# Seven block products for q G in a linear attention, added to x as their banks grow

## The chip, the cores and the metric

The kernel runs on one core of a Trainium2 chip. The metric is the device time of one execution in microseconds. An execution has five engines with queues of their own: PE (TensorE, matrix products, with a separate row PEld for its weight loads), DVE (VectorE), ACT (ScalarE), POOL (GpSimd) and SP (SyncE, which here issues DMAs).

## The reference

Four layers in a row on a tensor x of 2 batches, 1024 positions and 512 channels, each with a residual sum and a normalization of rows: a linear attention, a gated feed-forward network with 4-bit weights, a gated recurrent attention, and a routed feed-forward network. The change lies in the first layer, of which this is the core (16 heads of 32 channels):

```
q = elu(x Wq^T) + 1 ; k = elu(x Wk^T) + 1 ; v = x Wv^T     # per head
kv  = einsum('bhtd,bhte->bhde', k, v)
z   = 1 / (einsum('bhtd,bhd->bht', q, k.sum(axis=2)) + 1e-6)
out = einsum('bhtd,bhde,bht->bhte', q, kv, z)
x   = layernorm(x + out Wo^T)
```

## The kernel before, in words

Rows of x are cut into four blocks of 512 positions (blocks 0 and 1 are the first batch, 2 and 3 the second); a block is four tiles of 128 rows. All is float32. A tile of 128 rows by 512 columns fills one of the eight PSUM banks.

For each batch `b` the first stage does this. The products x Wk and x Wq of a block are made by `by_seven` (products at L316): a 2 x 2 partition of both operands, seven block products in place of eight, sums of operands on DVE (S1, S2, S3, and T1 to T4 by `sums_of_weights`, L302), and a bank `grow` into which several products are accumulated one after another, read between them. `elu1` (L271 to L273) makes elu + 1 with two passes on ACT and one on DVE. `add_xk` (L367) gathers k^T x in four banks over the two blocks of the batch. `values` (L417) and `G_rows` (L430) turn it into G, a 512 x 512 matrix for which out Wo^T = q G once the rows of q are weighed. `weigh` (L400 to L406) multiplies q's rows by z on DVE. `turned` transposes a weighed tile of q on PE (L197) and copies it to SBUF on ACT (L438). `add_o` multiplies that tile by G with four matmuls of 512 columns (L445), adds the bank to x on DVE (L453) and takes row statistics (L188, L189); after the fourth tile, `layernorm` normalizes the block on POOL (L183). A block of q G is thus four tiles.

Between these, `unpack_some` unpacks 4-bit weights of the second layer piece by piece: a DMA, two shift and mask operations on DVE (L237, L238), then one on ACT into `wgu` (L241) or on DVE into `wdn` (L245). 27 such pieces are spread over the stage. `split_some` transposes tiles of the finished block 0 (L197, `x1Tp`) and splits them in a high part on ACT (L211) and a low part on DVE (L212): the input of the second layer, whose matmuls begin at L632 (`gatep`, `upp`) when the first stage is over.

What runs between what is written by hand. `by_seven` is a generator that stops between products; `run` takes one list of other steps at each stop, and what is left after the last. PE's instructions are held in this written order (`behind`); the order on DVE, ACT and POOL comes from the framework's scheduler when the program is built, and each engine then goes through its instructions in that order. Banks come from rings: `rings["mm"]` (two banks during the stage), `rings["sum"]` (two), `rings["acc"]` (four), and `rings["free"]` for the splits, which is set to the `mm` ring before the last line of steps. The last steps of the stage, for block 3, stand outside of `run`:

```
rings["free"] = rings["mm"]
for more in turns(3, 0, 1) + split[3] + some_o(3, 0) + turns(3, 2) + some_o(3, 1) + turns(3, 3) + some_o(3, 2, 3):
    more()
```

Of the kernel before, what the change touches and what calls it, by code (L numbers as in the profile page):

```python
# [10 lines left out]
F32 = mybir.dt.float32  # L11
# [10 lines left out]
P = 128  # L22
B, T, C = 2, 1024, 512
NB = 4
KC = C // P
# [48 lines left out]
def body(ctx: ExitStack, tc: tile.TileContext, a: dict, out: bass.AP):  # L74
    nc = tc.nc
# [20 lines left out]
    def acc_bank(name):  # L96
        return bank("acc", name)
# [10 lines left out]
    def place_w(i, name):  # L108
        return wpool.tile([P, KC, C], F32, tag=f"A{i}", name=name)
# [4 lines left out]
    x_t = [x[:, :, :C] for x in x_row]  # L114
# [4 lines left out]
    def xT_slot(i, name, dtype=F32):  # L119
        return xtp.tile([P, KC, 512], dtype, tag=f"xT{i}", name=name)  # L120
# [55 lines left out]
    def layernorm(x, mv, eps=1e-5, by=nc.vector):  # L176

        n = x.shape[1]
        rs = sp.tile([P, 4], F32, tag="rs", name="rs")
        nc.vector.tensor_scalar_add(rs[:, :n], mv[:, :, 1], eps)  # L180
        power = nc.gpsimd.tensor_tensor(rs[:, :n], rs[:, :n], const("mhalf")[:, :n], ALU.pow).ins  # L181
        for i in range(n):
            by.tensor_scalar(x[:, i], x[:, i], mv[:, i, 0:1], rs[:, i : i + 1], ALU.subtract, ALU.mult)  # L183
        return power

    def row_stats(mv, x):
        st = sp.tile([P, 6], F32, tag="st", name="st")
        nc.vector.bn_stats(st, x)  # L188
        nc.vector.bn_aggr(mv, st)  # L189
# [98 lines left out]
    def behind():  # L288

        return ExitStack() if last_pe[0] is None else tc.issue_after(last_pe[0])  # L290
# [6 lines left out]
    def sums_of_weights(w, rooms):  # L297

        B11, B12, B21, B22 = (w[:, 2 * e : 2 * e + 2, 256 * o : 256 * o + 256] for e in range(2) for o in range(2))
        T1, T2, T4 = rooms  # L300
        for dst, x, y in ((T1, B12, B11), (T2, B22, T1), (T4, B21, T2), (B12, B22, B12)):
            nc.vector.tensor_sub(dst, x, y)  # L302
        return T1, T2, B12, T4

    def by_seven(x, w, T, rooms, pairs, ready):

        A11, A12, A21, A22 = (x[:, 2 * e : 2 * e + 2, 256 * t : 256 * t + 256] for t in range(2) for e in range(2))
        B11, B12, B21, B22 = (w[:, 2 * e : 2 * e + 2, 256 * o : 256 * o + 256] for e in range(2) for o in range(2))
        T1, T2, T3, T4 = T
        S1, S2, S3 = rooms  # L310

        def product(ps, a, b, first):
            with behind():
                for r in range(2):
                    for k in range(2):
                        ins = nc.tensor.matmul(  # L316
                            ps[:, 256 * r : 256 * r + 256], a[:, k, r * P : (r + 1) * P], b[:, k],
                            start=first and r == 0 and k == 0, stop=k == 1, skip_group_check=True,
                        ).ins
            last_pe[0] = ins  # L320
            return ps.rearrange("p (r c) -> p r c", r=2)

        nc.vector.tensor_add(S1, A21, A22)
        nc.vector.tensor_sub(S2, S1, A11)
        nc.vector.tensor_sub(S3, A11, A21)
        pairs.extend(new_pair(f"pair{t}") for t in range(2))
        c11, c12, c21, c22 = (pairs[t][:, :, 256 * o : 256 * o + 256] for t in range(2) for o in range(2))
        grow = bank("sum", "grow")
        p = product(grow, A11, B11, True)
        nc.scalar.copy(c11, p)  # L330
        yield
        p2 = product(mm_bank("P2"), A12, B21, True)
        nc.vector.tensor_add(c11, c11, p2)
        elu1(c11, c11)
        yield
        product(grow, S2, T2, False)
        nc.scalar.copy(c21, p)
        side = mm_bank("P7")
        p7 = product(side, S3, T3, True)
        nc.vector.tensor_sub(S2, A12, S2)  # L340
        yield
        product(grow, S1, T1, False)
        nc.scalar.copy(c22, p)
        nc.vector.tensor_add(c22, c22, p7)
        elu1(c22, c22)
        yield
        product(grow, S2, B22, False)
        elu1(c12, p)
        ready(0)
        product(side, A22, T4, False)  # L350
        nc.vector.tensor_add(c21, c21, p7)
        elu1(c21, c21)
        ready(1)
# [41 lines left out]
    def weigh(blk, t):  # L395

        for r in range(2):
            x = pairs_of["q", blk][t][:, r]
            e = wk.tile([P, C], F32, tag="e", name="qk")
            nc.vector.tensor_mul(e, x, ksum_of[blk // 2])  # L400
            z = sp.tile([P, 16], F32, tag="z", name="z", bufs=2)
            nc.vector.tensor_reduce(z, e.rearrange("p (h d) -> p h d", d=32), AX.X, ALU.add)
            nc.vector.tensor_scalar_add(z, z, 1e-6)
            nc.vector.reciprocal(z, z)
            x3 = x.rearrange("p (h d) -> p h d", d=32)
            nc.vector.tensor_mul(x3, x3, z.unsqueeze(2).to_broadcast([P, 16, 32]))  # L406

    vkm_of, qT, parts = {}, {}, []

    def values(b):  # L410

# [14 lines left out]
    def G_rows(b):  # L426
        for c in range(KC):
# [2 lines left out]
                last_pe[0] = nc.tensor.matmul(gp, vkm_of[b][:, c], Wo[:, c], start=True, stop=True).ins  # L430
            (nc.scalar.copy if c % 2 else nc.vector.tensor_copy)(G_of[b][:, c], gp)

    def turned(blk, i):
        with behind():
            pt = transposed(pairs_of["q", blk][i // 2][:, i % 2], "qTp", acc_bank)
        last_pe[0] = last_turned[0]
        t = qT[blk, i] = wk.tile([P, KC, P], F32, tag="qT", name="qT")
        nc.scalar.copy(t.rearrange("p k t -> p (k t)"), pt)  # L438

    def add_o(blk, i):  # L440

        ao = acc_bank("ao")
        with behind():
            for k in range(KC):
                ins = nc.tensor.matmul(  # L445
                    ao, qT[blk, i][:, k], G_of[blk // 2][:, k], start=k == 0, stop=k == KC - 1
                ).ins
        last_pe[0] = ins
        x = x_t[blk][:, i]
        if i == 0:  # L450
            mv_of[blk] = sp.tile([P, 4, 2], F32, tag="mv", name="mv")
        mv = mv_of[blk]
        nc.vector.tensor_add(x, ao, x)  # L453
        row_stats(mv[:, i], x)
        if i == 3 and blk < NB - 1:
            layernorm(x_t[blk], mv, by=nc.gpsimd)

    def split_some(*part):
        if 0 in part:
# [39 lines left out]
    def some_xk(blk, *part):  # L499
        return [lambda i=i: add_xk(blk, i) for i in part]  # L500

    def turns(blk, *part):
        return [lambda i=i: turned(blk, i) for i in part]

    def some_o(blk, *part):
        return [lambda i=i: add_o(blk, i) for i in part]

    job = lambda n: [lambda: unpack_some(n)]

    def k_products(blk):  # L510
        return by_seven(xT[blk], Wk, Ts["k"], S_rooms, pairs_of.setdefault(("k", blk), []), lambda t: sum_k(blk, t))

    def q_products(blk):
        return by_seven(xT[blk], Wq, Ts["q"], S_rooms, pairs_of.setdefault(("q", blk), []), lambda t: weigh(blk, t))

    step = lambda f, *x: [lambda: f(*x)]

    for b in range(B):
        i, j = 2 * b, 2 * b + 1
        if b:  # L520
            run(
                k_products(i),
                turns(1, 0, 1),
                some_o(1, 0) + turns(1, 2) + job(1) + some_o(1, 1) + turns(1, 3) + job(1),
                some_o(1, 2) + job(1), some_o(1, 3) + job(1), job(2),
            )
        run(k_products(j), [], some_xk(i, 0, 1) + job(2), some_xk(i, 2) + job(1), some_xk(i, 3) + job(1), job(1 + b))
        if b == 0:
            Ts["q"] = sums_of_weights(Wq, slices(wdn, 0, 3))
        else:  # L530

            Tq = place_w(1, "Tq")
            for n in range(3):
                nc.scalar.copy(Tq[:, n], wdn[:, n])
            Ts["q"] = (*slices(Tq, 0, 2), Ts["q"][2], *slices(Tq, 2, 3))
            S_rooms[0] = pieces_of(Tq[:, 3])
        run(
            q_products(i), [],
            some_xk(j, 0, 1) + job(1), some_xk(j, 2) + step(spread_ksum, b) + job(1), some_xk(j, 3) + job(1 + b),
        )  # L540
        if b == 0:
            xT[2] = load_xT(2)
        split = [step(split_some, n) if b else [] for n in range(4)]
        rings["free"] = (rings["sum"][(turn_of["sum"] + 1) % 2],)
        run(
            q_products(j),
            step(values, b),
            turns(i, 0, 1) + job(1 - b),
            step(G_rows, b) + split[0] + job(1 - b),
            some_o(i, 0) + turns(i, 2) + split[1] + some_o(i, 1) + turns(i, 3) + job(1 - b),  # L550
            some_o(i, 2) + split[2] + some_o(i, 3),
        )
        if b == 0:
            xT[3] = load_xT(3)
    rings["free"] = rings["mm"]
    for more in turns(3, 0, 1) + split[3] + some_o(3, 0) + turns(3, 2) + some_o(3, 1) + turns(3, 3) + some_o(3, 2, 3):
        more()
    late = mv_of[3]
    unpack_some(1000)
# [1025 lines left out]
```

## Time and profile before

| | us |
|---|---|
| median of 3 runs | 990.62 (990.50 to 990.67) |
| the profiled execution | 988.88 |
| its span in the profile | 987.1 |
| granted PE clock, mean | 0.998 |
| PE busy | 972.1 |
| DVE busy | 683.3 |
| the group q G (L445) on PE | 57.3 |

The span is what the profiler saw between the first and last instruction; 1.8 us of the execution lie outside of it. Busy time of an engine is the union of its instructions' durations; durations on PE overlap, so that the distance between starts tells more of a matmul's price than its duration. In the profile, one float32 matmul shows as two passes.

### The profile page before, as it was taken

The numbers are of one execution on the slowest core, as the hardware profiler recorded it, in microseconds if no ns is written. First come the engines' busy times: TensorE is split into PE (matmuls) and PEld (weight loads), VectorE is DVE, ScalarE is ACT, GpSimd is POOL, SyncE is SP. The second block draws the span as 40 slices with busy tenths as digits, with TensorE's granted clock in tenths as the row PEclk, the third lists the DMA queues.
The fourth block names the chain that finished last, engine by engine and source line by source line (L and its number), as shares of the span: only waits on it lengthen the run. The fifth ranks groups of instructions, "written<-read, shape, count | busy, mean of one in ns | idle before, by whom it ended". The sixth has DMA issues, their size and how long they took to land.

```text
span 987.1 us, 11453 instructions
## 1 busy us (share of the span) xinstructions
PE 972.1 (98%) x4253; PEld 745.1 (75%) x4253; DVE 683.3 (69%) x1291; ACT 288.4 (29%) x490; POOL 300.2 (30%) x276
## 2 busy tenths in 40 slices
PE   9999999999999999999999999999999999999996
PEld 6667666756888888888889655776768688888885
DVE  3568877867975686686672465466798795789644
ACT  2244333333542272263240432132220123220000
POOL 1110452004887265575565022002032011000022
PEclk9999999999999999999999999999999999999999
DMA  9632212100000000000020500000004302140011
GB/s 332 200 91 79 72 53 93 37 0 1 1 1 1 1 1 0 2 11 1 1 86 1 220 4 1 1 1 1 1 33 139 128 17 70 43 171 1 1 43 43
DMA packets 25979, 48.84 MB, mean 49 GB/s; under 512 B 4685, under 2 KB 6733, under 8 KB 25412
## 3 DMA queue, kind: packets, MB, share of 16 engines
q1 hardware_dynamic: 23139, 42.85, 13.1%
q0 software_dynamic: 1920, 4.22, 1.1%
q10 hardware_dynamic: 864, 1.05, 0.3%
q8 instruction: 33, 0.54, 0.2%
q14 instruction: 23, 0.18, 0.1%
HBM read 39.70 MB, written 10.52 MB: 51 GB/s over the span
## 4 chain that ended last, share of the span: by engine, by line
PE 84%; issue 8%; DVE 4%; POOL 2%; ACT 1%; DMA 1%; POOLq 0%; ACTq 0%; DVEq 0%
PE P L679 12%; PE yp L1329 9%; PE hp L1250 9%; PE gatep L632 8%; PE upp L632 8%; PE ao L445 6%; PE xk L367 6%; PE grow L316 5%; PE P L316 4%; PE ao L1133 3%; PE go L1089 2%; PE lp L595 1%; PE P L688 1%; PE kp L474 1%; PE up L1006 1%
## 5 line engine op out<-in xcount | busy, mean ns | idle before, releaser
L181 POOL TENSOR_TENSOR rs<-rs,table 128x4 f32<-128x4 f32 (+1 forms) x21 | 18.9, 902 | 327.9 <-DVE rs L180 327.6
L643 DVE SCALAR_TENSOR_TENSOR gate<-gatep,scale,gate 128x512 f32<-128x512 f32 x123 | 91.4, 743 | 7.4 <-PE gatep L632 6.9
L643 DVE SCALAR_TENSOR_TENSOR up<-upp,scale,up 128x512 f32<-128x512 f32 x112 | 83.1, 742 | 0.2
L632 PE MATMUL gatep<-x1Th,wgu 128*128 128x512 f32 x176 | 72.7, 413 | 0.0
L632 PE MATMUL upp<-x1Th,wgu 128*128 128x512 f32 x176 | 69.7, 396 | 0.0
L632 PE MATMUL gatep<-x1Tl,wgu 128*128 128x512 f32 x176 | 69.6, 395 | 0.0
L632 PE MATMUL upp<-x1Tl,wgu 128*128 128x512 f32 x176 | 69.5, 395 | 0.0
L679 PE MATMUL P<-wdn,h 128*128 128x256 f32 x256 | 60.5, 379 | 0.0
L832 POOL TENSOR_TENSOR h<-up,gate 128x512 f32<-128x512 f32 x30 | 38.6, 1287 | 70.4 <-ACT gate L831 65.3
L637 ACT ACTIVATE gate<-gatep,scale 128x512 f32<-128x512 f32 x41 | 28.3, 691 | 106.8 <-PE gatep L632 106.8
L445 PE MATMUL ao<-G,qT 128*128 128x512 f32 x128 | 57.3, 593 | 0.0
L1133 PE MATMUL ao<-W1o,uT 128*128 128x512 f32 x128 | 55.6, 592 | 0.0
L679 PEld LDWEIGHTS P<-wdn,h 128*128 128x128 f32 x256 | 48.5, 190 | 6.7
L1037 POOL TENSOR_TENSOR sum<-sum,sq 128x512 f32<-128x512 f32 x12 | 18.2, 1517 | 107.6 <-issue 83.7
L1133 PEld LDWEIGHTS ao<-W1o,uT 128*128 128x128 f32 x128 | 24.0, 190 | 28.7 <-issue 27.5
L188 DVE BATCH_NORM_STATS2 st<-x 128x6 f32<-128x512 f32 x64 | 42.7, 682 | 0.8
L367 PE MATMUL xk<-pair,x 128*128 128x512 f32 x96 | 42.7, 592 | 0.0
L445 PEld LDWEIGHTS ao<-G,qT 128*128 128x128 f32 x128 | 23.8, 190 | 24.3 <-issue 23.9
L632 PEld LDWEIGHTS upp<-x1Th,wgu 128*128 128x128 f32 x176 | 33.0, 188 | 9.3 <-DVE up L643 1.1
L632 PEld LDWEIGHTS upp<-x1Tl,wgu 128*128 128x128 f32 x176 | 33.1, 188 | 7.6
L632 PEld LDWEIGHTS gatep<-x1Th,wgu 128*128 128x128 f32 x176 | 33.1, 188 | 7.4 <-issue 0.3
L632 PEld LDWEIGHTS gatep<-x1Tl,wgu 128*128 128x128 f32 x176 | 33.1, 188 | 7.1
(405 smaller groups left out, 2239.5 us busy)
## 6 DMA issues: line engine op xcount, KB each, us to landing
pk<-in_gu SPq DMA_DIRECT2D x16, 352.0 KB, 3.7
x<-in_x SPq DMA_DIRECT2D x4, 1024.0 KB, 13.1
w<-in_w SPq DMA_DIRECT2D x1, 4096.0 KB, 16.1
xs<-picked SPq DMA_DIRECT2D x4, 1024.0 KB, 5.0
out<-x SPq DMA_DIRECT2D x4, 1024.0 KB, 4.3
w<-in_w SPq DMA_DIRECT2D x4, 1024.0 KB, 6.3
x0T<-in_xT SPq DMA_DIRECT2D x3, 1024.0 KB, 7.2
pk<-in_dn SPq DMA_DIRECT2D x11, 256.0 KB, 3.3
```

The lines of the kernel that those rows point to most:

```text
L188: nc.vector.bn_stats(st, x)
L316: ins = nc.tensor.matmul(ps[:, 256 * r : 256 * r + 256], a[:, k, r * P : (r + 1) * P], b[:, k], start=first and r == 0 and k == 0, stop=k ...
L367: ins = nc.tensor.matmul(acc_of[b][c], x_t[blk][:, i, c * P : (c + 1) * P], pairs_of["k", blk][i // 2][:, i % 2], start=blk % 2 == 0 and i ...
L445: ins = nc.tensor.matmul(ao, qT[blk, i][:, k], G_of[blk // 2][:, k], start=k == 0, stop=k == KC - 1).ins
L632: ins = nc.tensor.matmul(ps, wgu[:, k, at * P : (at + 1) * P], x[:, k], start=x is parts[0], stop=x is parts[1]).ins
L637: nc.scalar.activation(acc, ps, AF.Copy, scale=s)
L643: last = nc.vector.scalar_tensor_tensor(acc, ps, s, acc, ALU.mult, ALU.add).ins
L679: last_p[0] = nc.tensor.matmul(cut, x(j)[:, r], w[:, j], start=j == 0, stop=j == NP - 1 and tail is None).ins
L832: hm = nc.gpsimd.tensor_mul(h.chunk(f), up, gate).ins
L1133: nc.tensor.matmul(ao[i], uT[blk][:, k, i * P : (i + 1) * P], W1o[:, k], start=n == 0, stop=n == 3)
L1250: nc.tensor.matmul(ps[:, 256 * j : 256 * j + 256], w[:, k, 2 * g + j], x[:, k], start=k == 0, stop=k == 1)
L1329: nc.tensor.matmul(ps[:, 256 * r : 256 * r + 256], x(r, j), w(j), start=j == 0, stop=j == NJ - 1)
```

## The change

Blocks 0, 1 and 2 no longer multiply tile by tile. `turned` keeps q transposed for a whole block, in rooms of `wdn` that are unpacked later (blocks 0 and 1) or in a slot of `xT` (2 and 3). `o_products` then makes q G of the block from seven block products, as `by_seven` does, and adds the growing bank to x after each product: P1 goes to the upper left quarter of x, P1 + P6 to the lower left, and so on. `G_rows` also makes the sums of G. Block 3 stays with four tiles (`add_o`). The weighing of each batch's second block moves from inside its q products to steps after them, three of the four splits of block 0 move into the last line of steps, and unpacking pieces are placed anew.

```diff
     def sums_of_weights(w, rooms):
 
         B11, B12, B21, B22 = (w[:, 2 * e : 2 * e + 2, 256 * o : 256 * o + 256] for e in range(2) for o in range(2))
-        T1, T2, T4 = rooms
-        for dst, x, y in ((T1, B12, B11), (T2, B22, T1), (T4, B21, T2), (B12, B22, B12)):
+        T1, T2, T4, T3 = (*rooms, B12)[:4]
+        for dst, x, y in ((T1, B12, B11), (T2, B22, T1), (T4, B21, T2), (T3, B22, B12)):
             nc.vector.tensor_sub(dst, x, y)
-        return T1, T2, B12, T4
+        return T1, T2, T3, T4
...
@@ G_rows
             (nc.scalar.copy if c % 2 else nc.vector.tensor_copy)(G_of[b][:, c], gp)
 
+        room = wdn[:, 7:11] if b == 0 else place_w(3, "TG")
+        rooms = slices(room, 0, 3)
+        if b:
+
+            rooms.append(pieces_of(wk.tile([P, 512], F32, tag="qT3", name="T3", bufs=1)))
+        TG[b] = sums_of_weights(G_of[b], rooms), pieces_of(room[:, 3])
+
     def turned(blk, i):
+        if i == 0:
+            qT[blk] = wdn[:, 3:7] if blk < 2 else xT_slot(blk % 2, "qT")
...
-        t = qT[blk, i] = wk.tile([P, KC, P], F32, tag="qT", name="qT")
-        nc.scalar.copy(t.rearrange("p k t -> p (k t)"), pt)
+        nc.scalar.copy(qT[blk][:, :, tile_of(i)], pt.rearrange("p (k t) -> p k t", k=KC))
+
+    def o_products(blk):
+
+        A11, A12, A21, A22 = (qT[blk][:, 2 * e : 2 * e + 2, 256 * t : 256 * t + 256] for t in range(2) for e in range(2))
+        G = G_of[blk // 2]
+        B11, _, B21, B22 = (G[:, 2 * e : 2 * e + 2, 256 * o : 256 * o + 256] for e in range(2) for o in range(2))
+        (T1, T2, T3, T4), S1 = TG[blk // 2]
+        S2 = pieces_of(wk.tile([P, 512], F32, tag="qS", name="qS", bufs=1))
+
+        def product(ps, a, b, first, t, o):
+
+            with behind():
+                for r in range(2):
+                    for k in range(2):
+                        ins = nc.tensor.matmul(
+                            ps[:, 256 * r : 256 * r + 256], a[:, k, r * P : (r + 1) * P], b[:, k],
+                            start=first and r == 0 and k == 0, stop=k == 1, skip_group_check=True,
+                        ).ins
+            last_pe[0] = ins
+            x = x_t[blk][:, 2 * t : 2 * t + 2, 256 * o : 256 * o + 256]
+            nc.vector.tensor_add(x, x, ps.rearrange("p (r c) -> p r c", r=2))
+
+        nc.vector.tensor_add(S1, A21, A22)
+        nc.vector.tensor_sub(S2, S1, A11)
+        nc.vector.tensor_sub(A21, A11, A21)
+        grow = acc_bank("grow")
+        product(grow, A11, B11, True, 0, 0)
+        yield
+        product(acc_bank("P2"), A12, B21, True, 0, 0)
+        yield
+        product(grow, S2, T2, False, 1, 0)
+        nc.vector.tensor_sub(A12, A12, S2)
+        yield
+        side = acc_bank("P7")
+        product(side, A21, T3, True, 1, 1)
+        yield
+        product(grow, S1, T1, False, 1, 1)
+        yield
+        product(side, A22, T4, False, 1, 0)
+        yield
+        product(grow, A12, B22, False, 0, 1)
+        yield
+        mv = mv_of[blk] = sp.tile([P, 4, 2], F32, tag="mv", name="mv")
+        for i in range(4):
+            row_stats(mv[:, i], x_t[blk][:, i])
+        layernorm(x_t[blk], mv, by=nc.gpsimd)
+        yield
...
@@ the steps between products
         if b:
             run(
                 k_products(i),
-                turns(1, 0, 1),
-                some_o(1, 0) + turns(1, 2) + job(1) + some_o(1, 1) + turns(1, 3) + job(1),
-                some_o(1, 2) + job(1), some_o(1, 3) + job(1), job(2),
+                turns(1, 0, 1) + job(1), job(1),
+                turns(1, 2, 3) + some_o(1, 1) + job(1), some_o(1, 2) + job(1), some_o(1, 5) + job(1),
             )
...
         run(
-            q_products(i), [],
-            some_xk(j, 0, 1) + job(1), some_xk(j, 2) + step(spread_ksum, b) + job(1), some_xk(j, 3) + job(1 + b),
+            q_products(i, lambda t: weigh(i, t)), [],
+            some_xk(j, 0, 1) + job(1 + b), some_xk(j, 2) + step(spread_ksum, b) + job(1), some_xk(j, 3) + job(1 + b),
         )
...
         run(
-            q_products(j),
+            q_products(j, lambda t: None),
             step(values, b),
-            turns(i, 0, 1) + job(1 - b),
-            step(G_rows, b) + split[0] + job(1 - b),
-            some_o(i, 0) + turns(i, 2) + split[1] + some_o(i, 1) + turns(i, 3) + job(1 - b),
-            some_o(i, 2) + split[2] + some_o(i, 3),
+            turns(i, 0, 1) + split[0] + job(1 - b),
+            step(G_rows, b) + turns(i, 2, 3) + job(1 - b),
+            some_o(i, 3) + job(1 - b),
+            some_o(i, 1) + step(weigh, j, 0) + some_o(i, 3) + step(weigh, j, 1) + some_o(i, 1),
         )
...
     rings["free"] = rings["mm"]
-    for more in turns(3, 0, 1) + split[3] + some_o(3, 0) + turns(3, 2) + some_o(3, 1) + turns(3, 3) + some_o(3, 2, 3):
+    for more in (
+        split[1] + split[2] + split[3] + turns(3, 0, 1) + whole_o(0) + turns(3, 2) + whole_o(1) + turns(3, 3) + whole_o(2, 3)
+    ):
         more()
```

In the new step lists, `some_o(blk, n)` advances `o_products(blk)` by n stops, and `whole_o` calls `add_o` for tiles of block 3.

More of the change, by code (lines that the diff above doesn't have):

```diff
@@ L406, in weigh @@
             nc.vector.tensor_mul(x3, x3, z.unsqueeze(2).to_broadcast([P, 16, 32]))
-    vkm_of, qT, parts = {}, {}, []
+    vkm_of, qT, TG, o_of, parts = {}, {}, {}, {}, []
     def values(b):
@@ L445, in add_o @@
                 ins = nc.tensor.matmul(
-                    ao, qT[blk, i][:, k], G_of[blk // 2][:, k], start=k == 0, stop=k == KC - 1
+                    ao, qT[blk][:, k, tile_of(i)], G_of[blk // 2][:, k], start=k == 0, stop=k == KC - 1
                 ).ins
@@ L451, in add_o @@
             mv_of[blk] = sp.tile([P, 4, 2], F32, tag="mv", name="mv")
-        mv = mv_of[blk]
         nc.vector.tensor_add(x, ao, x)
-        row_stats(mv[:, i], x)
-        if i == 3 and blk < NB - 1:
-            layernorm(x_t[blk], mv, by=nc.gpsimd)
+        row_stats(mv_of[blk][:, i], x)
     def split_some(*part):
@@ L503, in turns, with some_o, one, whole_o @@
         return [lambda i=i: turned(blk, i) for i in part]
-    def some_o(blk, *part):
-        return [lambda i=i: add_o(blk, i) for i in part]
+    def some_o(blk, n):
+        def one():
+            if blk not in o_of:
+                o_of[blk] = o_products(blk)
+            next(o_of[blk])
+        return [one] * n
+    def whole_o(*part):
+        return [lambda i=i: add_o(3, i) for i in part]
     job = lambda n: [lambda: unpack_some(n)]
@@ L511, in k_products, with q_products @@
         return by_seven(xT[blk], Wk, Ts["k"], S_rooms, pairs_of.setdefault(("k", blk), []), lambda t: sum_k(blk, t))
-    def q_products(blk):
-        return by_seven(xT[blk], Wq, Ts["q"], S_rooms, pairs_of.setdefault(("q", blk), []), lambda t: weigh(blk, t))
+    def q_products(blk, ready):
+        return by_seven(xT[blk], Wq, Ts["q"], S_rooms, pairs_of.setdefault(("q", blk), []), ready)
     step = lambda f, *x: [lambda: f(*x)]
```

## The prediction, made before the changed kernel ran

> **What bounds the kernel now.** I read the page from its first part down: busy shares, then the chain that ended last, then the groups.
>
> ```profile
> PE 972.1 (98%) x4253; PEld 745.1 (75%) x4253; DVE 683.3 (69%) x1291; ACT 288.4 (29%) x490; POOL 300.2 (30%) x276
> ...
> PE 84%; issue 8%; DVE 4%; POOL 2%; ACT 1%; DMA 1%; POOLq 0%; ACTq 0%; DVEq 0%
> ...
> L445 PE MATMUL ao<-G,qT 128*128 128x512 f32 x128 | 57.3, 593 | 0.0
> ```
>
> PE is busy all the time and carries 84% of the chain. The group to be changed, the product q G of `add_o`, is 128 passes (64 matmuls, two passes each), with no idle time before it: each microsecond of it is on the path. Busy times overlap, so prices come from the spacing of starts in PE's timeline of the second batch's stage:
>
> ```profile
> 187.74 3.73 PE L417 MATMUL vk<-G,Wv 128*128 128x128 f32 x32
> ...
> 201.24 1.89 PE L316 MATMUL grow<-Tq 128*128 128x256 f32 x8
> 202.97 3.60 PE L445 MATMUL ao<-G,qT 128*128 128x512 f32 x8
> 206.40 0.60 PE L197 MATMUL qTp<-table,pair 128*128 128x128 f32 x4
> ...
> 211.15 1.89 PE L316 MATMUL grow<-Wq,rw 128*128 128x256 f32 x8
> 212.88 1.89 PE L316 MATMUL P<-Tq,x0T 128*128 128x256 f32 x8
> ...
> 231.22 7.03 PE L445 MATMUL ao<-G,qT 128*128 128x512 f32 x16
> ```
>
> There is no gap: a tile of q G takes 206.40 - 202.97 = 3.43 us, a block product of seven 202.97 - 201.24 = 1.73 us, four transposes 0.44 us. The stage ends at 231.22 + 6.87 = 238.1 us. Is there room beside PE? The timeline of DVE in the same stage:
>
> ```profile
> 72.81 1.28 DVE L400 TENSOR_TENSOR qk<-pair,ksum 128x512 f32<-128x512 f32 x2
> 74.01 1.27 DVE L402 TENSOR_REDUCE z<-qk 128x16 f32<-128x512 f32 x2
> ...
> 76.90 0.69 DVE L273 SCALAR_TENSOR_TENSOR pair<-pair,e 128x512 f32<-128x512 f32 x1
> ...
> 136.71 1.10 DVE L273 SCALAR_TENSOR_TENSOR pair<-pair,e 128x512 f32<-128x512 f32 x1 [1.70 <-ACT e L272]
> ...
> 214.37 0.69 DVE L273 SCALAR_TENSOR_TENSOR pair<-grow,e 128x512 f32<-128x512 f32 x1 [1.82 <-ACT e L272]
> ...
> 224.97 0.63 DVE L212 TENSOR_TENSOR x1Tl<-x1Tp,x1Th 128x512 fp32r<-128x512 f32 x1
> ```
>
> A full-tile operation costs DVE 0.60 us in a queue ((74.01 - 72.81)/2). Weighing two rows of q is six of these and four small ones and took 76.90 - 72.81 = 4.09 us, so a small one costs about 0.12 us. From 214.37 to 229.5 DVE has no gap at all: it is nearly as full there as PE, and the change gives it more.
>
> [...] At its end the last matmul stops at 978.65 us and the clock of the last 7 us averages 0.79; that is half clock for 2.9 us, so from 984.1 us, 5.4 us after. At its start, sixteen 128-column passes take 3.64 us (0.228 each, against 3.57/32 = 0.112 for `vk`). The first line is from PE's timeline, the second from the table of windows (busy time of PE, PE's loads, DVE, ACT, POOL, then clock, DMA share, GB/s):
>
> ```profile
> 1.04 3.64 PE L285 MATMUL idle<-ones 128*128 128x128 f32 x16 [1.04 <-DVE ones L281]
> ...
> 980.00:987.00 7.00, 0.00 (x0) 0.00 (x0) 1.37 (x5) 0.00 (x0) 2.58 (x3) 0.79 0.19 75
> ```
>
> [...] L273 above took 1.10 us at 136.71, while POOL normalized x, against 0.69 alone; at 121.89 an L340 with two SBUF inputs took 0.68 beside the same work.
>
> **The change, part by part.** Positions and waits below are those of the built program; durations are this trace's.
>
> *PE columns, blocks 0 to 2.* Four tiles at 3.43 (13.74 us) become seven products at 1.73 (12.09): -1.65 a block, **-4.95 us** in all. Block 3 keeps the four tiles. Transposes are as many as before.
>
> *DVE work added.* A block: seven adds to x in place of four, and four sums of q; a batch: four sums of G. That is 7 x 0.60 = 4.2 us a block and 2.4 a batch, 17.4 us of DVE. It costs nothing where PE has other work queued, but the growing bank makes it a wait: a product may not accumulate into `grow` before DVE has added the last partial sum to x.
>
> *Block 0 (88 to 105 us).* From DVE's 84.0 on I laid the new queue end to end: unpack halves 0.5, G copies, sums of G and q, then the add of the first product at 91.9 to 92.6. PE, 0.87 late through moved transposes, wants the third product at 92.2: it waits 0.45. The later adds end 0.1 us or more before they are wanted. **+0.45 us.**
>
> *Block 1 (105 to 133 us).* The block's sums of q stand behind the weighing, statistics and five unpack pairs. With 0.4 us more for each unpack half under POOL's normalization of x0 (seen at 116.62: 0.97 against 0.52), S2 is 0.25 late, and the add of P7 makes PE wait 1.1 us. Two-input sums now also run beside POOL's 9.5 us; half of some eight slowed by 0.4 gives more. I take **+2.0 us**; 0 if nothing is slowed, 4 if all are.
>
> *Jobs moved.* One unpack goes from the third block's k products to its q products: same 27 jobs, the same DMAs on SP's queue, all done before 190 us; in 160 to 180 us DVE is busy 13.5 of 20. POOL's normalizations of x0 and x1 start 2 us later and have until 200 us. q's room in `wdn` is free by 132 us, before its unpacking. Copies of q on ACT (0.59 each) are as many, just later. **0 us**; were this cover gone, one unpack pair is 0.9 us of DVE.
>
> *Block 2 and the tail (188 to 238 us).* Its first three products cost no wait (S2 at 205.1, the add at 206.9, wanted at 207.3). Weighing block 3 has moved behind q's last product, and three splits of x0 (L212, `split_some`) now stand together after the seven products. They draw on a ring of two banks: the third's transposes wait until DVE has done the first's L212. Ahead of that on DVE, from the elu of c12 (L273): two elu tails, one pair add, twelve full-tile operations of weighing, four adds to x, four statistics and L212 itself, 24 x 0.60 = 14.4, and eleven small ones, 1.3; with 0.2 of waiting for ACT, 15.9 us. The elu starts 214.37 - 212.88 = 1.49 us after PE's L316 `grow<-Wq,rw`, so DVE is there 17.4 us after it. PE from the same point: 1.73 + 4 x 1.73 + two splits 0.87 = 9.5, plus waits for adds of 0.2 and 1.0 in the queue (P7 and the fifth product). It stands from 10.7 to 17.4 us after that point: **+1.2 and +6.7 us**. Behind the wait stand the third split, the transposes of block 3 and its four tiles, 15.9 us, and then the whole next stage; in the kernel before, about half of those 15.9 us lay beside this DVE work. Block 3's first tile then waits for ACT's copy of its transposes, **+0.3**.
>
> *Clock.* 6.7 us of idleness exceeds the 5.4 above, so PE restarts at half speed. [...] I take **+1.4 us**[...].
>
> Sum: -4.95 + 0.45 + 2.0 + 1.2 + 6.7 + 0.3 + 1.4 = **+7.1 us**. Span 987.1 becomes 994.2, this execution's 988.88 becomes 996.0; the median, 990.62, lies 1.74 above that execution, so 997.7. Nothing later gives it back: PE has no gap in 240 to 300 us.
>
> **Rivals.** *A shorter queue.* Slowing by POOL is absent and DVE's queue is some 1.5 us shorter, so the idle stretch stays under 5.4 us and the clock full: -4.95 + 0.45 + 0.5 + 0.7 + 5.2 + 0.3 = +2.2, 992.8 us. For it: 0.6 us is an estimate from pairs, and 24 of them add up. Against: dependent neighbours cost 0.73 (206.60 to 207.33), which lengthens it. *Faster: PE decides alone.* If the third split gets its bank within the 10.7 us in which PE has work, the tail's wait is nil; with half of the smaller waits (0.45 + 2.0 + 1.2) hidden as well it is -4.95 + 1.8 = -3.1, 987.5 us, and 985.7 with all hidden. It would need DVE to pass the eleven small operations and the 24 full tiles in 10.7 - 1.5 = 9.2 us, 0.33 for a tile; the trace has none under 0.5 at this size and type. Only a wait that I attribute wrongly gives this. *The change doesn't do what it says:* seven products are in the built program's order, so I give this none.
>
> **How the numbers follow.** Long wait with half clock or nearly so: 0.68, 994.5 to 1001.5 us (no block-1 wait and no clock loss below[...]). Shorter queue: 0.19, 991 to 994.5. Faster: 0.10. No change: 0.03. 0.2%, 2 us, is about what a measurement can tell. Predicted 997.7, range 991 to 1002: it leaves the faster case out.
>
> **What would show it.** In the changed profile: products of `o_products` at 1.73 us each without `ao` in blocks 0 to 2; a PE gap of 5 to 8 us ended by DVE L212 before the third `x1Tp`; PE passes at double time just after it; a first `gatep` near 245 us instead of 238.1; small DVE-ended waits before grow products near 92, 120 and 127 us. Wrong: a tail with no gap, a gap that another engine ends, or a first `gatep` before 238.

## The result, and the profile after

The changed kernel takes **995.80 us** (median; 994.89 to 996.32) against 990.49 (990.05 to 990.67) for the kernel before beside it: ratio 1.0054, 95% interval 1.0043 to 1.0064. It is slower by 5.3 us. Forecast were 997.7 and "slower". The profiled execution has a span of 994.1 us. The first two lines are from its page, busy times and shares of the chain:

```profile
PE 970.7 (98%) x4325; PEld 760.7 (77%) x4325; DVE 696.2 (70%) x1320; ACT 287.5 (29%) x490; POOL 306.9 (31%) x276
...
PE 80%; issue 8%; DVE 7%; POOL 2%; ACT 2%; DMA 1%; POOLq 0%; ACTq 0%; DVEq 0%
```

PE has less work than before (972.1 there), DVE 12.9 us more, and the chain that ended last now runs through DVE for 7% instead of 4%: DVE has become a part of the path somewhere. PE's timeline in the second batch's stage says where (start, duration, instruction, and in brackets the idle time before it with what ended it):

```profile
202.79 1.89 PE L461 MATMUL grow<-G,qT 128*128 128x256 f32 x8
204.51 1.89 PE L461 MATMUL P<-G,qT 128*128 128x256 f32 x8
...
213.15 1.89 PE L461 MATMUL grow<-TG 128*128 128x256 f32 x8
215.17 1.99 PE L461 MATMUL P<-TG,qT 128*128 128x256 f32 x8
217.84 1.99 PE L461 MATMUL grow<-G,qT 128*128 128x256 f32 x8 [0.68 <-DVE x L467]
219.67 1.04 PE L197 MATMUL x1Tp<-table,x 128*128 128x128 f32 x8
227.17 1.12 PE L197 MATMUL x1Tp<-table,x 128*128 128x128 f32 x4 [6.46 <-DVE x1Tl L212]
228.08 1.92 PE L197 MATMUL qTp<-table,pair 128*128 128x128 f32 x8
229.81 4.26 PE L500 MATMUL ao<-G,qT 128*128 128x512 f32 x8
233.91 0.60 PE L197 MATMUL qTp<-table,pair 128*128 128x128 f32 x4
...
245.12 0.48 PE L694 MATMUL gatep<-x1Th,wgu 128*128 128x512 f32 x1
```

Products start 1.73 us apart where nothing waits (as between 202.79 and the next). The two starts after 213.15 are 2.02 and 2.67 apart: 0.29 and 0.94 late, and the splits at 219.67 come another 0.10 late. Two splits take 0.87, so PE stands from 220.54 to 227.17: 6.63 us. (The bracket has 6.46, because it counts from the modelled end of the last transpose.) What it waits for is in DVE's timeline:

```profile
211.19 0.69 DVE L273 SCALAR_TENSOR_TENSOR pair<-grow,e 128x512 f32<-128x512 f32 x1 [2.33 <-ACT e L272]
...
217.11 0.68 DVE L467 TENSOR_TENSOR x<-x,grow 128x512 f32<-128x512 f32 x1
...
226.44 0.67 DVE L212 TENSOR_TENSOR x1Tl<-x1Tp,x1Th 128x512 fp32r<-128x512 f32 x1
```

From the elu at 211.19 to the end of L212 at 227.11 lie 15.92 us of DVE's queue. Between them DVE's timeline shows one pause, of 0.18. L212 is what empties the first split's bank; PE's third split starts 0.06 us after it. The table of windows shows the clock (columns: busy us and count of PE, PE's loads, DVE, ACT, POOL, then granted clock, DMA share, GB/s):

```profile
220.00:225.00 5.00, 0.71 (x7) 0.47 (x5) 5.00 (x14) 2.56 (x4) 0.00 (x0) 0.91 0.00 0
225.00:230.00 5.00, 2.83 (x13) 2.61 (x14) 3.54 (x9) 1.17 (x2) 1.96 (x2) 0.50 0.00 0
230.00:232.00 2.00, 2.00 (x4) 0.96 (x5) 0.00 (x0) 0.59 (x1) 2.00 (x2) 0.76 0.00 0
```

A mean of 0.91 over 5 us is half clock for 0.9 us: it fell near 224.1, 3.6 us after PE went idle, and by the last window came back near 231.0, 3.8 us after PE's restart. At half clock four transposes took 0.91 us instead of 0.44, eight took 1.73 instead of 0.87, and the `ao` tile 4.10 instead of 3.43: 2.0 us.

**The whole account.** The executions do not start alike: PE's second group of `kp` waits for a DMA at the very start, and begins at 8.29 us here against 6.73 before, 1.56 us that are no part of the change. (I call this the start's offset and take it from every position.) `vk`, which opens the second batch's stage, starts at 186.69 against 187.74; less the offset, the first batch saves 2.61 us. From `vk` to the first `gatep` it is 58.43 us against 50.38: 8.05 lost. 8.05 - 2.61 = 5.44, and the medians differ by 5.31.

### The profile page after: what moved, and what is told of

Its sections match the earlier page's. It is cut to its first block, busy times and chain, and to the rows that moved or that the text cites. A ratio compares the mean times of both kernels' runs of the same rounds, so it can differ in the third digit from the quotient of the medians.

```text
span 994.1 us, 11631 instructions
## 1 busy us (share of the span) xinstructions
PE 970.7 (98%) x4325; PEld 760.7 (77%) x4325; DVE 696.2 (70%) x1320; ACT 287.5 (29%) x490; POOL 306.9 (31%) x276
## 4 chain that ended last, share of the span: by engine, by line
PE 80%; issue 8%; DVE 7%; POOL 2%; ACT 2%; DMA 1%; POOLq 0%; ACTq 0%; DVEq 0%
PE P L741 12%; PE yp L1391 9%; PE hp L1312 9%; PE upp L694 8%; PE gatep L694 8%; PE xk L367 5%; PE grow L316 4%; PE P L316 3%; PE ao L1195 3%; PE go L1151 2%; PE grow L461 2%; PE ao L500 1%; PE lp L657 1%; PE P L750 1%; PE kp L526 1%
## 5 line engine op out<-in xcount | busy, mean ns | idle before, releaser
L181 POOL TENSOR_TENSOR rs<-rs,table 128x4 f32<-128x4 f32 (+1 forms) x21 | 20.3, 968 | 323.0 <-DVE rs L180 322.7
L1391 PE MATMUL yp<-w,h 128*128 128x256 f32 x168 | 37.7, 379 | 0.0
L741 PE MATMUL P<-T,S 128*128 128x256 f32 x160 | 35.8, 379 | 0.0
```

The lines of the kernel that those rows point to most:

```text
L741: last_p[0] = nc.tensor.matmul(cut, x(j)[:, r], w[:, j], start=j == 0, stop=j == NP - 1 and tail is None).ins
L1391: nc.tensor.matmul(ps[:, 256 * r : 256 * r + 256], x(r, j), w(j), start=j == 0, stop=j == NJ - 1)
```

## Experiments

Theory: seven products save PE 4.95 us of columns as counted; most of the loss is the in-order wait for one bank, 6.6 us, and the half clock after it, 2.0. Rivals: the added work of DVE costs as much wherever the splits stand; the clock has nothing to do with the gap; POOL beside DVE has a price of its own. Each run is given as its ratio to the kernel before on the same chip. Differences in us to the changed kernel are between medians of different sets of runs, in which the kernel before took from 989.73 to 990.49 us; they are rough to about half a microsecond, and where that matters the traces are compared, from `vk` to the end of block 3's tiles (the last `ao` start plus 6.87 us: 58.40 us in the changed kernel).

| run | edit | ratio, 95% interval |
|---|---|---|
| e1_ring | four banks for the splits | 0.9973 [0.9963, 0.9984] |
| e2_order | two banks, third split later | 0.9991 [0.9984, 0.9997] |
| e3_weigh | half of block 3's weighing left out | 1.0012 [1.0004, 1.0020] |
| e4_fill | idle matmuls in the gap | 1.0034 [1.0022, 1.0046] |
| e5_first | seven products in the first batch alone | 0.9977 [0.9967, 0.9987] |
| e7_nopool | x0, x1 not normalized | 1.0069 [1.0055, 1.0083] |
| e6_best | four banks, adds before weighing | 0.9995 [0.9987, 1.0004] |
| e6b_late_split | four banks, third split later | 0.9970 [0.9958, 0.9983] |
| e8_second_only | as e6b, adds earlier in the second batch | 0.9971 [0.9961, 0.9982] |

**Is the gap the ring of two banks?**

```diff
-    rings["free"] = rings["mm"]
+    rings["free"] = (*rings["mm"], *rings["sum"])
```

> The changed kernel, but the last three splits of block 0 draw on four banks (the mm ring and the sum ring) in place of two, so that the third needs no bank that DVE still has to read. Theory (the two-bank ring behind DVE's long queue costs the tail): the third x1Tp follows the second without a gap, the gap of 6.6 us goes and with it the half clock after it (2.0 us), the wait for ACT's copy of q (0.3) comes back: 8.3 us less, 987.5 us, so some 3 us below the kernel before. Rival 1 (DVE's amount of work binds there, whatever the bank): the wait only moves to the next transposes of q, which need the weighed rows; 994 to 996 us. Rival 2 (seven products with adds to x are slower in themselves): the same 994 to 996 us.

Measured: 987.82 us, 2.6 below the kernel before, 8.0 below the change. DVE does the same work in both. PE's timeline:

```profile
217.43 1.99 PE L461 MATMUL grow<-G,qT 128*128 128x256 f32 x8 [0.68 <-DVE x L467]
219.26 1.47 PE L197 MATMUL x1Tp<-table,x 128*128 128x128 f32 x12
220.57 1.04 PE L197 MATMUL qTp<-table,pair 128*128 128x128 f32 x8
222.00 3.70 PE L500 MATMUL ao<-G,qT 128*128 128x512 f32 x8 [0.40 <-ACT qT L446]
225.54 0.60 PE L197 MATMUL qTp<-table,pair 128*128 128x128 f32 x4
```

Three splits run without a stop, and the granted clock is 1.00 in every window from 205 to 245; the add wait of block 2 stays; the wait for ACT, which the gap had hidden, is there at 0.40 in the bracket. By spacing of starts the tile is 0.56 late and its successor another 0.11. The gap and its clock without these are 6.63 + 2.0 - 0.67 = 7.96; the medians differ by 8.0. This shows the cause: the ring of two banks, not DVE's load as such.

**Or the order?** Two banks stay; only the place of the third split is another.

```diff
-        split[1] + split[2] + split[3] + turns(3, 0, 1) + whole_o(0) + turns(3, 2) + ...
+        split[1] + split[2] + turns(3, 0, 1) + whole_o(0) + split[3] + turns(3, 2) + ...
```

> The changed kernel with its two banks, but the third split stands behind the first tile of block 3 in PE's order, as a split did in the kernel before. Theory: PE has 0.9 us of transposes and a tile of 3.4 us before it needs the bank; of the 6.6 us of gap some 1.9 remain, too short for the clock to fall: 6.3 us less, 989.5 us. Rival 1 (DVE's work binds whatever the bank): 994 to 996 us. Against the variant with four banks it should be 2 us longer.

Measured: 989.41 us. PE now has block 3's first tile to do while it would have stood:

```profile
226.82 0.65 PE L197 MATMUL x1Tp<-table,x 128*128 128x128 f32 x4 [1.55 <-DVE x1Tl L212]
```

The split starts where it did (less the offsets, 225.66 here and 225.61 in the changed kernel), because DVE's L212 sets it, but of the gap 1.55 us are left, and the granted clock is 1.00 in every window from 205 to 245. So what the change lost was the work queued behind a split that could not start. It is 1.6 us longer than e1, as these 1.55 us say. This and e1 are two cures for one wait.

**Does DVE's queue set the gap's length, and the gap the clock?** The weighing of block 3's second pair of rows is left out.

```diff
-            some_o(i, 1) + step(weigh, j, 0) + some_o(i, 3) + step(weigh, j, 1) + some_o(i, 1),
+            some_o(i, 1) + step(weigh, j, 0) + some_o(i, 3) + (step(weigh, j, 1) if b == 0 else []) + some_o(i, 1),
```

> The changed kernel without the weighing of the last two row tiles of block 3 (these rows of q stay undivided): six full-tile operations and four small ones less in DVE's queue ahead of the first split's L212, two banks as before. Theory (length of DVE's queue sets the gap): the gap shrinks by 4.1 us to 2.5, and as it is now shorter than what the clock needs to fall, the 2.0 us of half clock go as well: 990 us. Rival 3 (something else than DVE's queue frees the bank, such as ACT's cast): no change, 995.8 us. Rival 4 (half clock has nothing to do with the gap's length): 991.7 us.

Measured: 991.75 us: what the rival wrote. But the trace shows another reason than the rival's. PE's timeline, then the windows:

```profile
217.96 1.04 PE L197 MATMUL x1Tp<-table,x 128*128 128x128 f32 x8
222.20 0.87 PE L197 MATMUL x1Tp<-table,x 128*128 128x128 f32 x4 [3.20 <-DVE x1Tl L212]
222.87 1.91 PE L197 MATMUL qTp<-table,pair 128*128 128x128 f32 x8
```

```profile
215.00:220.00 5.00, 3.32 (x19) 2.43 (x17) 4.18 (x9) 1.28 (x3) 0.00 (x0) 1.00 0.00 0
220.00:225.00 5.00, 2.80 (x14) 2.79 (x15) 3.58 (x11) 1.35 (x3) 1.93 (x2) 0.75 0.00 0
225.00:230.00 5.00, 5.00 (x14) 2.37 (x14) 0.98 (x2) 1.11 (x3) 5.00 (x3) 0.91 0.00 0
```

The gap is 222.20 - 218.83 = 3.37 us instead of 6.63, shorter by 3.3 where I wrote 4.1: with less in its queue DVE itself waits for PE's last product (4.18 us busy of 5 in the first window, 4.82 there in the changed kernel). That part of the theory holds. And 3.37 us of idleness were enough: the clock was at half for 2.5 us of one window and 0.9 of the next, about 222.5 to 225.9. My threshold of 5.4 us was wrong. By the traces this run is 3.4 us shorter than the changed kernel (55.00 against 58.40), by the medians 4.05; that the median fell on the rival's number is chance.

**What is the clock alone worth?** Idle matmuls of ones into an unused bank, between the second and third split, keep PE busy in the gap and shorten nothing.

```diff
+    def filling():
+        room = bank("sum", "filling")
+        with behind():
+            for _ in range(28):
+                ins = nc.tensor.matmul(room[:, :P], ones, ones, start=True, stop=True).ins
+        last_pe[0] = ins
...
-        split[1] + split[2] + split[3] + turns(3, 0, 1) + ...
+        split[1] + split[2] + step(filling) + split[3] + turns(3, 0, 1) + ...
```

> The changed kernel with 28 idle matmuls of ones (128 columns, 0.22 us each, 6.2 us in all) into an unused bank between the second and the third split; they wait for nothing and nobody needs them. Theory (idleness makes PE fall to half clock): the wait for DVE stays as it is, but the passes after it keep their full rate: 2.0 us less, 0.3 of it given back to the wait for ACT's copy: 994.1 us. Rival 4 (the double time after the gap is not the clock): 995.8 us or more.

Measured: 994.05 us.

```profile
220.26 6.42 PE L620 MATMUL filling<-ones 128*128 128x128 f32 x56
226.88 0.66 PE L197 MATMUL x1Tp<-table,x 128*128 128x128 f32 x4 [0.21 <-DVE x1Tl L212]
...
228.70 3.70 PE L500 MATMUL ao<-G,qT 128*128 128x512 f32 x8 [0.21 <-ACT qT L446]
```

Less its offset of 1.22 the split starts at 225.66 again, the tile's successor starts 232.24 - 228.70 = 3.54 us after it, and the granted clock stays at full rate where the changed kernel had 0.91 and 0.50:

```profile
220.00:225.00 5.00, 5.00 (x47) 5.00 (x46) 5.00 (x15) 2.56 (x4) 0.00 (x0) 1.00 0.00 0
225.00:230.00 5.00, 4.58 (x31) 3.56 (x31) 3.26 (x8) 1.70 (x4) 2.25 (x2) 1.00 0.00 0
```

The medians fall by 1.75, the traces by 1.37 (57.03 against 58.40). The latter is the 2.0 of half clock less the waits for ACT and DVE that the slow passes had hidden: 0.45 ahead of the tile, 0.17 in smaller ones.

**Which batch has the gain?** The first batch as changed, the second as before:

```diff
     def G_rows ...
+        if b:
+            return
...
+        if b:
+            run(
+                q_products(j, lambda t: weigh(j, t)),
+                ...
+                tiles_o(i, 0) + turns(i, 2) + split[1] + tiles_o(i, 1) + turns(i, 3),
+                tiles_o(i, 2) + split[2] + tiles_o(i, 3),
+            )
+        else: ...
```

> Seven products in the first batch alone (blocks 0 and 1, with the changed kernel's steps there); the second batch has the steps of the kernel before: block 2 in four tiles, weighing of block 3 inside its q products, the splits spread between tiles. Theory (the products themselves pay, the tail does not): in the changed kernel's trace two blocks of products saved 2.6 us by the start of the second batch's last q products, and nothing after it takes that back: 990.5 - 2.6 = 987.9 us. Rival 2 (products with adds to x are no faster): 990.5 us. Rival 5 (the saving is eaten later, in the stage bound by both PE and DVE): 989 to 990.5 us.

Measured: 987.24 us, 2.5 below before. `vk` starts at 185.60, 0.43 of it offset: 2.57 saved, as in the changed kernel. The rest of the stage takes 50.37 us, as before. The two batches are separate accounts: the first gains 2.6 us, the second loses 8.05.

**Does POOL's normalization cost PE anything in block 1?** I had priced it at 2.0 us. The changed kernel shows no wait of PE there. The normalization of x0 and x1 is left out:

```diff
-        layernorm(x_t[blk], mv, by=nc.gpsimd)
+        if blk == 2:
+            layernorm(x_t[blk], mv, by=nc.gpsimd)
```

> The changed kernel without POOL's normalization of x0 and x1 (blocks 0 and 1 go on unnormalized). Theory (POOL beside DVE costs nothing in block 1, since DVE's adds there are on time by themselves): the same time, 995.8 us, with DVE's slowed operations near 121 to 131 us back at their usual length. Rival (the 2.0 us that the prediction put on this are paid somewhere that the profile does not show as a wait): 993.8 to 995.3 us.

Measured: 996.57 us, a ratio of 1.0069 where the changed kernel has 1.0054: no faster, and their intervals overlap. PE's timeline has even gained a wait, and DVE's shows why:

```profile
130.55 1.99 PE L461 MATMUL grow<-G,wdn 128*128 128x256 f32 x8 [0.29 <-DVE x L467]
```

```profile
128.13 1.16 DVE L325 TENSOR_TENSOR b<-x0T 128x512 f32<-128x512 f32 x1
...
130.41 1.27 DVE L237 TENSOR_SCALAR pk<-pk,shift 128x704 int32<-128x704 int32 x1
```

L325 is slow here, 1.16 us against 0.67 to 0.71 for its neighbours, ahead of the add that PE wants; in the changed kernel L325 was slow (1.75, at 130.99) only behind that add, beside POOL's sums of k (L386, from 130.76). Here POOL, with nothing to normalize, waited 70.1 us for an elu of DVE (L273) and then came to its sums of k, near 126.5: my estimate from those 70.1 us and from the elu that ended at 126.39. That these are what slowed L325 I argue from their place in time, not from a run without them. `vk` saves 1.97 instead of 2.61; the product at 130.55 is 0.51 late by spacing and its successor another 0.10, which is that difference. So the run recovered no hidden price, but it put a new wait in: it is no clean test, and that block 1 paid nothing is better seen in the changed kernel's own trace.

**Can both kernels be beaten?** First all at once: four banks, adds of both second blocks ahead of the weighing, splits behind block 3's first transposes.

```diff
-            some_o(i, 1) + step(weigh, j, 0) + some_o(i, 3) + step(weigh, j, 1) + some_o(i, 1),
+            some_o(i, 4) + step(weigh, j, 0) + step(weigh, j, 1) + some_o(i, 1),
...
-    rings["free"] = rings["mm"]
+    rings["free"] = (*rings["mm"], *rings["sum"])
...
-        split[1] + split[2] + split[3] + turns(3, 0, 1) + whole_o(0) + turns(3, 2) + ...
+        turns(3, 0) + split[1] + split[2] + split[3] + whole_o(0) + turns(3, 1, 2) + ...
```

> The variant with four banks for the splits, and two things more: adds to x of a block stand before the weighing of the next in the written steps, and block 3's first transposes go ahead of the three splits, so that ACT copies them while PE splits. Theory: the two waits for adds in block 2 (0.3 and 0.9 us) shrink to the first, and the wait for ACT's copy (0.4) goes: 987.8 - 1.3 = 986.5 us. Rival: the weighing that now comes later on DVE is waited for in its turn by block 3's transposes: 987.5 to 989 us.

A miss: 989.54 us. `vk` starts at 188.00, 0.27 of it offset, so the first batch saves nothing. PE's timeline has three waits that the changed kernel has not:

```profile
108.14 0.63 PE L197 MATMUL qTp<-table,pair 128*128 128x128 f32 x4 [0.71 <-DVE z L403]
...
120.49 1.99 PE L461 MATMUL grow<-wdn,qS 128*128 128x256 f32 x8 [0.48 <-DVE qS L470]
...
131.94 1.99 PE L461 MATMUL grow<-G,wdn 128*128 128x256 f32 x8 [0.83 <-DVE x L467]
```

By spacing of starts they are 0.87, 0.65 and 0.99: 2.5 us, which is what is missing. With adds first, block 1's first rows of q are weighed late: DVE's weighing of its first two tiles of q (L406) ends at 107.99 here and at 108.02 in the changed kernel; less the offsets of 0.27 and 1.56 that is 1.26 us later. That is the first wait. Ahead of each of the other two, DVE's timeline has an operation that is slow beside POOL: L469 took 1.09 us at 118.30, while POOL normalized x0, and L273 took 1.75 at 129.53, while POOL summed k (L386, from 128.97 to 130.74); others like them took 0.68. At 0.68 each, an estimate from these figures, 0.24 of the second wait would be left and nothing of the third. So about half of the loss comes with operations slowed beside POOL; no run separates it from the new order.

Then without the moved adds, and with the third split behind two transposes of block 3:

```diff
-        split[1] + split[2] + split[3] + turns(3, 0, 1) + whole_o(0) + ...
+        split[1] + split[2] + turns(3, 0, 1) + split[3] + whole_o(0) + ...
```

> The variant with four banks, with only one thing more: the third split stands behind block 3's first two transposes, to cover ACT's copy. Theory: the wait of 0.40 us for ACT's copy goes and nothing else: 987.4 us. Rival: DVE is what PE waits for there, not ACT: 987.8 us.

Measured: 986.78 us, the lowest ratio, 0.9970: faster than both kernels, though its interval overlaps those of e1 and e5. The split covers ACT's copy, and the tile follows only 0.07 late:

```profile
220.66 0.60 PE L197 MATMUL x1Tp<-table,x 128*128 128x128 f32 x4
221.17 3.70 PE L500 MATMUL ao<-G,qT 128*128 128x512 f32 x8
```

Last, this version with the adds moved in the second batch alone:

```diff
-            some_o(i, 1) + step(weigh, j, 0) + some_o(i, 3) + step(weigh, j, 1) + some_o(i, 1),
+            (some_o(i, 4) if b else some_o(i, 1)) + step(weigh, j, 0) + ([] if b else some_o(i, 3)) + step(weigh, j, 1) + some_o(i, 1),
```

> Of the eighth variant, only the second batch keeps the new place of the adds: four stops of the products of block 2 come before both weighings, while the first batch keeps the order of the changed kernel; the four-bank ring and the third split behind block 3's first two transposes are as in the run with the late split. Theory: the moved adds were good in the second batch and bad in the first, where the second pair of weighed q rows is wanted by PE two products after its elu. So the first batch saves 2.6 us again (vk at 185.1 plus the luck of the start), and in block 2 the 0.27 + 0.68 us that its last two products waited for DVE's adds are gone: 0.9 us below the late split's 0.9970 of the kernel before, so a ratio of 0.996, about 986 us. PE may wait up to 0.4 us for ACT's copies of block 3's transposes, since weighing comes later: 0.996 to 0.9965. Rival: the first batch loses its 2.6 us whatever the place of the adds in the first batch, since the larger ring shifts DVE's queue: then about 0.9990.

Measured: 987.28 us, 0.9971: the rival is out (`vk` at 186.43, 1.26 of it offset, saves 2.57), and so is the further gain. PE's timeline:

```profile
216.75 1.89 PE L461 MATMUL grow<-G,qT 128*128 128x256 f32 x8
...
219.35 0.60 PE L197 MATMUL qTp<-table,pair 128*128 128x128 f32 x4
220.96 0.63 PE L197 MATMUL qTp<-table,pair 128*128 128x128 f32 x4 [1.01 <-DVE z L403]
```

The wait for the add is gone (216.75 carries none), and the weighing, now later, is waited for instead, by 1.0 us (1.17 by spacing of starts). From `vk` to the end of block 3's tiles it is 50.05 us, against 49.96 with the late split. The wait has only changed its place: DVE is full in this stretch (4.82 and 5.00 of 5 us in the changed kernel's windows from 215 and from 220), and whichever of its results comes last is the one that PE waits for.

## Why the prediction was right, and where not

The direction, the mechanism and its place were right, and the time is in the range. One term, block 1, was mis-sized. Term by term, predicted and measured in the traces, in us:

| term | predicted | measured |
|---|---|---|
| columns, three blocks | -4.95 | -4.95 |
| block 0, waits for adds | +0.45 | +0.68 |
| block 1, waits behind POOL's work | +2.0 | 0 |
| block 2, waits for adds | +1.2 | +1.33 |
| wait for the bank | +6.7 | +6.63 |
| ACT's copy, and half clock | +1.7 | +2.0 |
| waits of the kernel before that went | none | -0.25 |
| sum | +7.1 | +5.44 |

The measured sum is the 5.44 of the whole account above; the medians have 5.31.

*Columns.* Products start 1.73 us apart with no `ao` among them in blocks 0 to 2. e6b closes the account: 4.95 + 0.25, less 0.68 in block 0, 1.34 in block 2 and 0.18 at its first tile of block 3, leaves 3.0; it measured 2.95.

*Block 0.* The first wait stands where it was put (predicted wish 92.2, start 92.65; here, less the offset, 92.61):

```profile
92.03 1.89 PE L461 MATMUL P<-G,wdn 128*128 128x256 f32 x8
94.17 1.99 PE L461 MATMUL grow<-wdn,qS 128*128 128x256 f32 x8 [0.25 <-DVE x L467]
96.00 1.89 PE L316 MATMUL grow<-Wq,rw 128*128 128x256 f32 x8
...
129.01 1.89 PE L461 MATMUL P<-wdn 128*128 128x256 f32 x8
130.73 1.89 PE L461 MATMUL grow<-G,wdn 128*128 128x256 f32 x8
132.46 1.89 PE L316 MATMUL grow<-Wk,x0T 128*128 128x256 f32 x8
```

The start at 94.17 is 0.41 late by its neighbour and the next one another 0.10; two more, at 104.70 and 106.54, are 0.06 and 0.11 late. That is 0.68, and 3.30 of columns less 0.68 is what the first batch saved.

*Block 1: the mis-sized term.* The last three lines above are its last products, 1.73 apart: no wait. Two steps failed: "0.4 us more for each unpack half", on which the late S2 and the 1.1 us of wait at the add of P7 rested, and "half of some eight slowed by 0.4". The timelines of POOL and DVE of the changed kernel:

```profile
118.49 11.63 POOL L183 TENSOR_SCALAR x<-x,mv,rs 128x512 f32<-128x512 f32 x4
...
122.24 0.81 DVE L238 TENSOR_SCALAR pk<-pk 128x704 int32<-128x704 int32 x1
```

POOL's four tiles took 11.63 us against 9.50 before. Of DVE's operations beside them two of six unpack halves rose, to 0.81, and four stayed at 0.51 to 0.58; the two-input ones stayed at 0.67 to 0.69. So here POOL lost more than DVE. DVE was busy for 11.50 of these 11.63 us, and for 8.42 of the 9.50 before, from where I had taken the price. That the fuller queue is what put the loss on POOL is a guess of mine that no run shows: in e6 and e7 single two-input operations of DVE were slow beside POOL (1.09, 1.75 and 1.16 us). The add of P7 ended at 128.77 and its successor in that bank was wanted at 129.01: 0.24 us of margin. That the term came to nothing was in part luck of position: in e6 PE did wait in block 1, 0.65 us for S2 and 0.99 for a late add, behind such slow operations.

*Block 2 and the bank.* The waits for adds were 0.29 and 0.94, and 0.10 at the start after them. The queue laid end to end (15.9 us, from 1.49 after PE's product to 17.4) measured 15.92, and L212 ended 227.11 - 209.69 = 17.42 after it. PE's own work from there was 10.85 us, 10.7 in the prediction. One name was wrong in it: the product from which it counts (212.88 before, 209.69 after) is `P<-Tq,x0T`, the one after `grow<-Wq,rw`; the numbers are those of the right product.

*Waits of the kernel before.* "There is no gap" missed two small ones, in PE's timeline of the kernel before:

```profile
223.22 3.67 PE L445 MATMUL ao<-G,qT 128*128 128x512 f32 x8
226.85 0.66 PE L197 MATMUL qTp<-table,pair 128*128 128x128 f32 x4
227.34 3.60 PE L445 MATMUL ao<-G,qT 128*128 128x512 f32 x8
```

The first two starts are 3.63 apart and the next two 0.49, where a tile takes 3.43 and four transposes 0.44: 0.25 us that the changed kernel does not have.

*DVE's added work.* The 29 added operations are there (1320 against 1291), but busy time rose by 12.9 us, not 17.4. Why is open; the waits above were counted from the queue and do not rest on it.

*Clock.* Half clock came, at 2.0 us instead of 1.4, and the 0.3 for ACT's copy was not seen beside it. The 1.4 rested on an estimate of mine for how long half clock lasts; PE worked 3.8 us at it. The threshold under it was wrong: 5.4 us, from the end of the trace before. Here the fall came 3.6 us after the last transposes. The rival "a shorter queue" kept the clock full through 5.2 us of idleness; e3, where the clock fell with 3.37 us of idleness, shows that it would not have. Another reading stays open: at the start of the trace before the passes take double time for 3.47 us (1.04 to 4.51), but the table of windows gives a granted clock of 1.00 for these microseconds, so only the durations speak for half clock there.

*Signs.* The products, the gap ended by L212 and the double time after it came as forecast. The first `gatep` at 245.12 looks like the forecast 245, but that is luck: 1.56 of it is the start's offset, and the change itself moved it by 5.44 and not by 7. No wait came near 120 or 127.

The prediction is 1.9 us too high: 1.8 in the change (7.1 against 5.3), and 0.1 because the median of before was 990.62 in one set of runs and 990.49 in the other. Block 1 was 2.0 too high and the waits of the kernel before were left out (0.25); block 0, block 2 and the clock were too low by 0.2, 0.1 and 0.3, which hid a part of it.

## What to carry to other kernels

Cutting PE work pays only as far as the engine that takes over the sums has room where the sums are wanted; count its queue from the last thing that releases it to the one result that PE stops for. When steps are regrouped, count the banks of the ring that they share: three takers in a row on two banks made an in-order engine wait 6.6 us for work far down another queue, two more banks turned a loss of 5.3 us into a gain of 2.6, other work ahead of the third taker into one of 1.0, and four banks with a later third split gained 2.95. Once the other engine is full, changing the order of its results can move the wait rather than remove it, as in e8 (1.01 us of waiting for the weighing in place of 0.68 for the add).

## What the runs showed of the hardware

- The clock can fall though the gap is over. In e3 PE was idle for 3.37 us, and the windows put the fall near 222.5, 0.3 us after PE had restarted; in the changed kernel it fell 3.6 us after PE went idle. It stayed low for 3.4 us in e3 and for some 6.9 in the changed kernel, of which PE worked 3.8. After PE's last work the fall came 3.1 us later at the end of the changed kernel's trace (the last matmul ends at 985.66, the windows put the fall near 988.74), 3.6 in its gap, 3.7 in e3 (222.5 - 218.83) and 5.4 at the end of the trace before, so these four lie 2.3 us apart. After the 1.55 us of e2 the clock stayed at 1.00.
- Twenty-eight idle matmuls in the gap were worth 1.75 us by the medians and 1.4 by the traces, just by keeping the clock.
- In the changed kernel POOL, beside a full DVE queue (busy 11.50 of 11.63 us), lost 2.1 us in four tiles and another 1.4 in one tiny operation (L181, 2.47 us against 1.06), and this cost the path nothing. In e6 and e7, with queues as full but for pauses of 0.34 and 0.21 us, single two-input operations of DVE took 1.09, 1.75 and 1.16 us beside POOL where others took 0.68, and PE waited for what stood behind them. Which side loses was not settled by how full the queue is.
